# One exponential over two score banks, and one PSUM tile for seven banks, in the last attention of a four-layer kernel

## The chip, the core and the metric

The kernel runs on one core of a Trainium2 chip. Five engines matter: TensorE (products and transpositions, "PE" in the profile; its weight loads are "PEld"), VectorE ("DVE"), ScalarE ("ACT"), GpSimd ("POOL") and SyncE ("SP", which issues the transfers). TensorE writes into PSUM, which has eight banks of 512 fp32 columns on each of 128 partitions; VectorE and ScalarE read from it. The engines run side by side and wait for each other through semaphores. The metric is the device time of one execution in microseconds (us).

## What is computed

The reference takes x (16 sequences of 128 tokens, 256 features) through four layers, each an attention and a feed-forward part, both added to x. The change lies in the last layer, whose attention looks from every one of the 2048 tokens to all 2048 tokens of a context, with 16 heads of width 16 and integer-rounded q, k, v and weights:

```
attn = jnp.einsum('bhqd,bhkd->bhqk', q, k)
attn = jax.nn.softmax(attn.astype(jnp.float32), axis=-1)
attn = _fq_unsigned(attn, axis=-1)          # max/255 is the step; round to 0..255
out = jnp.einsum('bhqk,bhkd->bhqd', attn, v)
...
out = jnp.einsum over the experts: silu(x @ gate) * (x @ up) @ down, the best two of 8, and a shared one
```

The kernel gets the rounding to 0..255 by subtracting the row's maximum, adding log 255, and letting the exponential be written out as an integer.

## The kernel before

The first three layers and the keys and values of the fourth run up to about 1834 us. Then `l3` runs the last attention and the last mixture of experts together.

The work is cut into *units*: unit `u` is one tile of 128 queries and one head, 16 tiles of 16 heads, 256 in all. A unit has four *pieces* of scores, 128 x 512 each, one PSUM bank each. For a unit the steps are:

- `scores` (L967): a product per piece, TensorE.
- `peak` (L973): the negated maximum of each piece, VectorE, into a column of `nm`; `bias` (L978, L979) makes the unit's bias `nb` of the four.
- `exponentials` (L991): four exponentials, ScalarE, from the pieces' banks into the integer tile `p`, each with its sum into a column of `z`. In the profile an exponential is an ACTIVATE and an ACTIVATION_READ_ACCUMULATOR.
- `turn_p` (L1004): 16 transpositions of `p`, eight to a bank; the first eight are copied out by VectorE (L1006), the others by ScalarE (L1008).
- `values` (L1017): 16 products into the bank `av`, which is apart from the others.

Eight banks are used: one for `av`, and seven, `b0` to `b6`, for all else in the stage. `take` gives out the bank that was free longest by a hand-set due time, `give` returns it with such a time. Each take makes a new tile in the bank's own place.

The order on the engines is written out by hand (`tc.manual_schedule`): the loop over `u` issues the exponentials of `u`, pieces 2 and 3 of `u + 1` with their maxima, the transpositions of `u - 1`, the values of `u - 2`, and pieces 0 and 1 of `u + 2` with theirs. Between these stand the pieces of the rest. Ten units of each tile carry an `expert`: a gate-and-up product (L243, `gu`), two passes of ScalarE (L1192 and L1193), and `rest`, a pass of VectorE (L1196) and one of GpSimd (L1197). The table `steps` places the others (norm, projection of q, its rounding and transposition, output projection, gate, the experts' transpositions `turn_a` and `down` products) at the end of fixed units; what they read back from PSUM is put off to the middle of the next unit's exponentials (`mid`) or maxima (`between`).

The wait that an instruction gets comes from its tiles: the framework sees which tiles it reads and writes, and sets semaphores so that it comes after the earlier users of those tiles.

Of the kernel before, what the change touches and what calls it, by code (L numbers as in the profile page):

```python
# [18 lines left out]
F32 = mybir.dt.float32  # L19
# [5 lines left out]
AF = mybir.ActivationFunctionType  # L25
ALU = mybir.AluOpType
AX = mybir.AxisListType
PSUM = bass.MemoryType.PSUM

P = 128  # L30
NT = 16
D = 256
NH = 16
# [7 lines left out]
class Net:  # L41
# [879 lines left out]
    def l3(self, w3, moe_w):  # L921
# [7 lines left out]
        nc, tc = self.nc, self.tc  # L929
# [5 lines left out]
        with (self.pool("l3x", bufs=2) as pool, self.pool("l3p", bufs=3) as pp,  # L935
              self.pool("l3t", bufs=LAG + 1) as tp, self.pool("l3m", bufs=1) as mp,
              self.pool("l3e", bufs=3) as ep):
            st = {}

            banks = {f"b{j}": float(j - 7) for j in range(7)}  # L940

            def take(shape, name, dtype=F32):
                tag = min(banks, key=banks.get)
                del banks[tag]
                return self.bank(shape, tag, name, dtype), tag

            def give(tag, when):
                banks[tag] = when
# [10 lines left out]
            def flush(which, u):  # L959
                for f in which.pop(u, ()):  # L960
                    f()


            def scores(u, q):
                t, hd = divmod(u, NH)
                ps, tag = st["s", u, q] = take([P, 512], "piece")
                nc.tensor.matmul(ps, qTs[t % 2][:, hd, :],  # L967
                                 kst[q // 2][:, hd // 2, 512 * (q % 2):512 * (q % 2) + 512], start=True, stop=True)

            def peak(u, q):  # L970
                if q == 0:
                    st["nm", u] = self.s(4, "nm")
                nc.vector.tensor_reduce(st["nm", u][:, q:q + 1], st["s", u, q][0], AX.X, ALU.max, negate=True)  # L973

            def bias(u):
                t, hd = divmod(u, NH)
                nb = st["nb", u] = self.s(1, "nb")
                nc.vector.tensor_reduce(nb, st.pop(("nm", u)), AX.X, ALU.min)  # L978
                nc.vector.tensor_scalar(nb, nb, st["sq", t][:, hd:hd + 1], LN255, ALU.mult, ALU.add)  # L979

            def exponentials(u):
                t, hd = divmod(u, NH)
                if hd == 0:
                    st["z", t] = pool.tile([P, NH, 4], F32, name="z", tag="z")

                p, nb = pp.tile([P, T], I16, name="p", tag="p"), st.pop(("nb", u))
                for q in range(4):
                    if q == 2:
                        flush(mids, u)
                    ps, tag = st.pop(("s", u, q))  # L990
                    nc.scalar.activation(p[:, 512 * q:512 * q + 512], ps, AF.Exp, bias=nb,  # L991
                                         scale=st["sq", t][:, hd:hd + 1], accum_out=st["z", t][:, hd, q:q + 1])
                    give(tag, u + (0.2, 0.4, 0.6, 0.8)[q])
                st["p", u] = p

            def turn_p(u, half, now):

                if half == 0:
                    st["pT", u] = tp.tile([P, NT, P], I16, name="pT", tag="pT")
                p, out = st["p", u].bitcast(BF16), st["pT", u][:, 8 * half:8 * half + 8, :]  # L1000
                ps, tag = take([P, 8, P], "pTp", BF16)
                for j in range(8):
                    n = (8 * half + j) * P
                    nc.tensor.transpose(ps[:, j, :], p[:, n:n + P], self.identb)  # L1004
                if half == 0:
                    nc.vector.tensor_copy(out, ps.bitcast(I16))  # L1006
                else:
                    nc.scalar.copy(out.rearrange("p j q -> p (j q)").bitcast(F32), ps.rearrange("p j q -> p (j q)").bitcast(F32))  # L1008
                give(tag, now + (0.9 if half == 0 else 1.0))

            def values(u):
                t, hd = divmod(u, NH)
                if hd == 0:
                    st["av", t] = self.bank([P, NH, 16], "av", "av")
                pb = st.pop(("pT", u)).bitcast(F16)
                for c in range(NT):
                    nc.tensor.matmul(st["av", t][:, hd, :], pb[:, c, :], v[:, c, hd * 16:(hd + 1) * 16],  # L1017
                                     start=(c == 0), stop=(c == NT - 1))
# [168 lines left out]
            def expert(e):  # L1187
                def step(t, u):
                    ps, tag = take([P, 2 * IN], "gu")
                    self.matmul_acc(ps, [(st["mhT"][:, c, :], wgu[:, c, e, :]) for c in range(2)])  # L1190
                    a, b = (ep.tile([P, IN], F32, name=n, tag=n) for n in ("ma", "mb"))
                    nc.scalar.activation(a, ps[:, :IN], AF.Tanh, scale=0.5)  # L1192
                    nc.scalar.activation(b, ps[:, IN:], AF.Identity, scale=st["comb"][:, e:e + 1])  # L1193

                    def rest():
                        nc.vector.scalar_tensor_tensor(a, a, 1.0, ps[:, :IN], ALU.add, ALU.mult)  # L1196
                        nc.gpsimd.tensor_tensor(act[:, e * IN:(e + 1) * IN], a, b, ALU.mult)  # L1197
                        give(tag, u + 0.95)
                    return rest
                return step  # L1200
# [30 lines left out]
            N = NT * NH  # L1231
# [4 lines left out]
            with tc.manual_schedule(engines={E.PE, E.DVE, E.Activation, E.Pool, E.SP}):  # L1236
                nc.gpsimd.memset(act[:, NE * IN:], 0.0)
                nc.vector.tensor_scalar(sv, sv, 2.0 ** 24, None, ALU.mult)
                for qT in qTs:
                    nc.gpsimd.memset(qT, 0.0)  # L1240
                for n in sorted(n for n in steps if n < 0):
                    for f in steps[n]:
                        f(0, -2)
                        flush(mids, -1)
                        flush(betweens, -1)
                for q in range(4):
                    scores(0, q)
                    peak(0, q)
                bias(0)
                for q in range(2):  # L1250
                    scores(1, q)
                    peak(1, q)
                for u in range(N + 33):
                    if u < N:
                        exponentials(u)
                    else:
                        flush(mids, u)

                    rest = None
                    for q in (2, 3):  # L1260
                        if u + 1 < N:
                            scores(u + 1, q)
                            peak(u + 1, q)
                        if q == 2:
                            flush(betweens, u)
                            for t in range(NT):
                                if FIRST <= u - NH * t < FIRST + NE:
                                    rest = expert(u - NH * t - FIRST)(t, u)
                    if u + 1 < N:
                        bias(u + 1)  # L1270

                    if 0 <= u - 1 < N:
                        for half in range(2):
                            turn_p(u - 1, half, u)
                    if 0 <= u - LAG < N:
                        values(u - LAG)
                        if (u - LAG) % NH == NH - 1:
                            divide((u - LAG) // NH, u)
                    for q in range(2):
                        if u + 2 < N:  # L1280
                            scores(u + 2, q)
                    if rest:
                        rest()
                    for q in range(2):
                        if u + 2 < N:
                            peak(u + 2, q)

                    for t in reversed(range(NT)):
                        for f in steps.get(u - NH * t, ()) if u - NH * t >= 0 or t > 0 else ():
                            f(t, u)  # L1290


    def run(self):
        self.load_x()
        late = ExitStack()
        self.l0(late)
        with self.pool("w3", 1) as self.w:
            w3 = self.l3_weights()
            self.middle(w3)
            late.close()  # L1300
            with self.pool("w4", 1, "right") as self.w:
                moe_w = self.moe_weights("L3_ffn", 10)
                with self.psum(av=1, **{f"b{j}": 1 for j in range(7)}):
                    self.l3(w3, moe_w)


# [67 lines left out]
```

## Time and profile before

| | |
|---|---|
| three runs | 3094.66, 3092.42, 3086.54 us; median 3092.42 |
| profiled execution | 3084.17 us, span 3082.5 us, mean granted TensorE clock 0.958 |
| TensorE products, weight loads | busy 2613.2 us (85%), 1772.8 us (58%) |
| VectorE | busy 2116.1 us (69%) |
| ScalarE | busy 1893.2 us (61%) |
| GpSimd | busy 1060.0 us (34%) |
| DMA | 12 GB/s on average |

The busy shares are means over the whole span, with stages of different limits in it. The last stage, from 1834 us, has its own balance, and is to be read by a window. Rows of the profile give line, engine, operation, output<-input, shapes and count; then busy us and mean ns of one, then the idle time before it and whose end ended it. PEclk is the clock that TensorE was granted, 1.00 at full speed.

### The profile page before, as it was taken

What the parts mean: (1) busy time and instruction counts of PE and PEld (TensorE: products, weight loads), DVE (VectorE), ACT (ScalarE), POOL (GpSimd) and SP (SyncE); (2) the same over time, 40 slices, a digit from 0 to 9 for tenths busy, and PEclk for the clock granted to TensorE, in tenths of its full rate; (3) what the DMA queues carried; (4) which work ended last, traced back from release to release, by engine and by line L of the source; (5) the groups of instructions that cost most, each with busy time, mean ns of one, the idle gap of its engine ahead of it and who ended that gap; (6) DMA issues with size and microseconds to landing.
All of it is one profiled execution on the core that took longest, in us unless ns stands there. A gap on an engine that the chain in (4) does not pass through costs nothing.

```text
span 3082.5 us, 50232 instructions
## 1 busy us (share of the span) xinstructions
PE 2613.2 (85%) x18166; PEld 1772.8 (58%) x18166; DVE 2116.1 (69%) x5254; ACT 1893.2 (61%) x4908; POOL 1060.0 (34%) x1683
## 2 busy tenths in 40 slices
PE   5889999999998877888888857788888888888888
PEld 3556666666665544555555534555555555555556
DVE  5655565656657435667666539888888888888884
ACT  1344444444444325555555429988888888888895
POOL 4544443444443315555555420222222222222212
PEclk9899999999998988999999979999999999999999
DMA  5000000000001010000000010000000000000000
GB/s 200 1 1 1 1 1 1 1 1 1 1 1 53 21 54 5 5 4 5 5 4 3 1 71 1 2 3 3 3 3 3 3 3 3 3 3 3 3 3 6
DMA packets 27385, 37.68 MB, mean 12 GB/s; under 512 B 6432, under 2 KB 23424, under 8 KB 26368
## 3 DMA queue, kind: packets, MB, share of 16 engines
q1 hardware_dynamic: 27136, 34.47, 3.4%
q8 instruction: 143, 2.34, 0.3%
q14 instruction: 106, 0.87, 0.1%
HBM read 32.37 MB, written 2.10 MB: 11 GB/s over the span
## 4 chain that ended last, share of the span: by engine, by line
PE 53%; DVE 19%; ACT 17%; POOL 6%; issue 5%; DMA 1%; ACTq 0%; SPq 0%; DVEq 0%; POOLq 0%
ACT p L991 10%; PE gu L243 9%; PE tp L219 6%; DVE nm L973 5%; PE pTp L1004 4%; PE oproj L549 4%; PE q L243 4%; PE scores L273 4%; PE moe L1214 3%; PE av L289 3%; PE piece L967 3%; PE moe L243 2%; PE oT L541 2%; DVE pT L1006 2%; PE out L243 2%
## 5 line engine op out<-in xcount | busy, mean ns | idle before, releaser
L991 ACT ACTIVATE p<-piece,nb,hs 128x512 int16<-128x512 f32 x1024 | 789.4, 785 | 8.1 <-DVE nb L979 8.1
L973 DVE TENSOR_REDUCE nm<-piece 128x1 f32<-128x512 f32 x1024 | 661.6, 683 | 141.5 <-PE piece L967 138.8
L967 PE MATMUL piece<-kst,qT 128*128 128x512 bf16 x1024 | 351.5, 383 | 127.2 <-DVE pT L1006 96.7
L1004 PEld LDWEIGHTS <-p 128*128 128x128 bf16 x4096 | 257.8, 98 | 193.2 <-issue 160.6
L1004 PE MATMUL pTp<-identb,p 128*128 128x128 bf16 x4096 | 294.5, 220 | 51.6 <-ACT p L991 28.5
L243 PE MATMUL gu<-w_L_ffn_wgu,mhT 128*128 128x352 f32 x640 | 223.2, 474 | 21.4 <-ACT p L991 19.1
L1197 POOL TENSOR_TENSOR act<-ma,mb 128x176 f32<-128x176 f32 x160 | 89.5, 559 | 421.3 <-DVE ma L1196 390.7
L235 ACT COPY pT<-tp 128x512 f32<-128x512 f32 (+1 forms) x208 | 116.0, 563 | 181.0 <-PE tp L219 180.0
L1008 ACT COPY pT<-pTp 128x512 f32<-128x512 f32 x256 | 150.0, 586 | 107.7 <-PE pTp L1004 107.7
L991 ACT ACTIVATION_READ_ACCUMULATOR p<-piece,nb,hs 128x1 f32 x1024 | 214.1, 209 | 0.0
L270 POOL TENSOR_TENSOR kx<-kT,hmask 128x512 f32<-128x512 f32 x128 | 132.9, 1047 | 146.0 <-PE scores L273 94.4
L534 ACT ACTIVATE s<-s,nb,qs 128x128 f32<-128x128 f32 x256 | 123.2, 482 | 97.4 <-DVE nb L532 95.9
L289 PEld LDWEIGHTS av<-v,pT 128*128 128x128 f32 x1024 | 132.4, 197 | 87.1 <-ACT pT L235 73.6
L1006 DVE COPY pT<-pTp 128x1024 int16<-128x1024 int16 x256 | 174.3, 681 | 1.4 <-PE pTp L1004 1.4
L243 PE MATMUL gu<-w_L_ffn_wgu,hT 128*128 128x352 f32 x512 | 174.5, 463 | 0.9 <-ACT actT L235 0.6
L289 PE MATMUL av<-v,pT 128*128 128x17 f32 x1024 | 133.7, 262 | 47.8 <-ACT pT L235 47.7
L243 PEld LDWEIGHTS gu<-w_L_ffn_wgu,mhT 128*128 128x128 f32 x640 | 111.9, 189 | 101.7 <-ACT p L991 63.5
L280 ACT ACTIVATE p<-scores,mx,qs 128x128 f32<-128x128 f32 x256 | 96.9, 459 | 118.7 <-DVE mx L278 111.1
L967 PEld LDWEIGHTS <-qT 128*128 128x128 bf16 x1024 | 91.8, 98 | 130.8 <-issue 104.6
L275 DVE TENSOR_REDUCE mx<-scores 128x4 f32<-128x512 f32 x128 | 88.2, 689 | 114.0 <-PE scores L273 113.5
L273 PE MATMUL scores<-kx,qT 128*128 128x512 f32 x256 | 152.2, 679 | 3.1 <-ACT qT L235 2.7
L1179 POOL TENSOR_SCALAR gw<-gtop,gden 128x2 f32<-128x2 f32 x16 | 4.2, 263 | 417.3 <-DVE gden L1178 417.3
(367 smaller groups left out, 5973.3 us busy)
## 6 DMA issues: line engine op xcount, KB each, us to landing
w_L_ffn_wgu<-in_L_ffn_wgu SPq DMA_DIRECT2D x1, 3520.0 KB, 11.7
w_L_ffn_wgu<-in_L_ffn_wgu SPq DMA_DIRECT2D x1, 2816.0 KB, 11.3
x<-in_x SPq DMA_DIRECT2D x16, 128.0 KB, 4.2
ctxT<-in_ctxT SPq DMA_DIRECT2D x4, 512.0 KB, 5.1
w_L_ffn_qT<-in_L_ffn_qT SPq DMA_DIRECT2D x1, 2048.0 KB, 12.2
w_L_ffn_oT<-in_L_ffn_oT SPq DMA_DIRECT2D x1, 2048.0 KB, 17.5
ctx<-in_ctx SPq DMA_DIRECT2D x16, 128.0 KB, 2.0
out<-x SPq DMA_DIRECT2D x16, 128.0 KB, 1.7
```

The lines of the kernel that those rows point to most:

```text
L219: nc.tensor.transpose(ps[:, j, :], src[:, (j0 + j) * P:(j0 + j + 1) * P], self.ident)
L243: self.nc.tensor.matmul(ps, a, b, start=(j == 0), stop=(j == n - 1))
L270: nc.gpsimd.tensor_tensor(kx, kT[oc].unsqueeze(1).to_broadcast([P, 4, P]), self.hmask[:, hs].unsqueeze(2).to_broadcast([P, 4, P]), ALU.mult)
L273: nc.tensor.matmul(ps, qT[:, oc, :], kx, start=True, stop=True)
L289: nc.tensor.matmul(av[:, 4 * g + h, :], pT[:, h, :], v[:, 4 * g + h, :], start=True, stop=True)
L549: nc.tensor.matmul(proj, oT[:, j, :], w["o"][:, c, :], start=(c == 0), stop=(c == 15))
L967: nc.tensor.matmul(ps, qTs[t % 2][:, hd, :], kst[q // 2][:, hd // 2, 512 * (q % 2):512 * (q % 2) + 512], start=True, stop=True)
L973: nc.vector.tensor_reduce(st["nm", u][:, q:q + 1], st["s", u, q][0], AX.X, ALU.max, negate=True)
L991: nc.scalar.activation(p[:, 512 * q:512 * q + 512], ps, AF.Exp, bias=nb, scale=st["sq", t][:, hd:hd + 1], accum_out=st["z", t][:, hd, q:q ...
L1004: nc.tensor.transpose(ps[:, j, :], p[:, n:n + P], self.identb)
L1006: nc.vector.tensor_copy(out, ps.bitcast(I16))
L1008: nc.scalar.copy(out.rearrange("p j q -> p (j q)").bitcast(F32), ps.rearrange("p j q -> p (j q)").bitcast(F32))
```

## The change

The seven banks become one tile, `seven`, of 7 x 512 columns; `take` gives out slices of it, numbered 0 to 6. With that, a pair of pieces can be one operand even where its two banks do not touch: `pair` makes an access pattern over banks `a` and `b` with step `abs(a - b)`. A unit's exponentials become two, of 1024 columns each, over pieces 0 and 1 and over pieces 2 and 3; the maxima of pieces 0 and 1 become one; pieces 2 and 3 keep one each. Where the first piece of a pair lies in the higher bank, the pair is read in the other order, and `turn_p` turns the two halves in the other order to make up for it.

```diff
-            banks = {f"b{j}": float(j - 7) for j in range(7)}
+            seven = self.bank([P, 7, 512], "seven", "piece")
+            banks = {j: float(j - 7) for j in range(7)}
 
             def take(shape, name, dtype=F32):
                 tag = min(banks, key=banks.get)
                 del banks[tag]
-                return self.bank(shape, tag, name, dtype), tag
+                ps = seven[:, tag, :]
+                if dtype != F32:
+                    ps = ps.bitcast(dtype)
+                n = shape[1] * (shape[2] if len(shape) == 3 else 1)
+                ps = ps[:, :n]
+                return ps.rearrange("p (j q) -> p j q", q=shape[2]) if len(shape) == 3 else ps, tag
+
+            def pair(u, q):
+
+                a, b = st["s", u, q][1], st["s", u, q + 1][1]
+                return seven[:, min(a, b):max(a, b) + 1:abs(a - b), :], a < b
...
             def peak(u, q):
                 if q == 0:
-                    st["nm", u] = self.s(4, "nm")
-                nc.vector.tensor_reduce(st["nm", u][:, q:q + 1], st["s", u, q][0], AX.X, ALU.max, negate=True)
+
+                    st["nm", u] = self.s(3, "nm")
+                    nc.vector.tensor_reduce(st["nm", u][:, :1], pair(u, 0)[0], AX.XY, ALU.max, negate=True)
+                else:
+                    nc.vector.tensor_reduce(st["nm", u][:, q - 1:q], st["s", u, q][0], AX.X, ALU.max, negate=True)
...
-                    st["z", t] = pool.tile([P, NH, 4], F32, name="z", tag="z")
+                    st["z", t] = pool.tile([P, NH, 2], F32, name="z", tag="z")
 
                 p, nb = pp.tile([P, T], I16, name="p", tag="p"), st.pop(("nb", u))
-                for q in range(4):
+                for q in (0, 2):
                     if q == 2:
                         flush(mids, u)
-                    ps, tag = st.pop(("s", u, q))
-                    nc.scalar.activation(p[:, 512 * q:512 * q + 512], ps, AF.Exp, bias=nb,
-                                         scale=st["sq", t][:, hd:hd + 1], accum_out=st["z", t][:, hd, q:q + 1])
-                    give(tag, u + (0.2, 0.4, 0.6, 0.8)[q])
+                    ps, st["first", u, q // 2] = pair(u, q)
+                    nc.scalar.activation(p[:, 512 * q:512 * q + 1024].rearrange("p (a n) -> p a n", a=2), ps, AF.Exp,
+                                         bias=nb, scale=st["sq", t][:, hd:hd + 1],
+                                         accum_out=st["z", t][:, hd, q // 2:q // 2 + 1])
+                    for k in (0, 1):
+                        give(st.pop(("s", u, q + k))[1], u + (0.3, 0.31, 0.7, 0.71)[q + k])
...
                 ps, tag = take([P, 8, P], "pTp", BF16)
+                first = st.pop(("first", u, half))
                 for j in range(8):
-                    n = (8 * half + j) * P
+                    n = (8 * half + (j if first else (j + 4) % 8)) * P
                     nc.tensor.transpose(ps[:, j, :], p[:, n:n + P], self.identb)
...
                 for q in range(4):
                     scores(0, q)
+                for q in (0, 2, 3):
                     peak(0, q)
                 bias(0)
                 for q in range(2):
                     scores(1, q)
-                    peak(1, q)
+                peak(1, 0)
...
-                    for q in range(2):
-                        if u + 2 < N:
-                            peak(u + 2, q)
+                    if u + 2 < N:
+                        peak(u + 2, 0)
...
-                with self.psum(av=1, **{f"b{j}": 1 for j in range(7)}):
+                with self.psum(av=1, seven=1):
                     self.l3(w3, moe_w)
```

In the changed kernel the lines are: pieces L978, maxima L985 (pair) and L987, bias L992 and L993, exponentials L1005, transpositions L1021 with their copies L1023 and L1025, values L1034, the expert's passes L1209, L1210 and L1213.

## The prediction

> **What bounds the kernel now.** The page's first two parts give the whole. Then the windows view cuts out the stage that the change touches, from 1834 us (the first score product starts at 1835.8) to the end, 1248.5 us.
>
> ```profile
> span 3082.5 us, 50232 instructions
> PE 2613.2 (85%) x18166; PEld 1772.8 (58%) x18166; DVE 2116.1 (69%) x5254; ACT 1893.2 (61%) x4908; POOL 1060.0 (34%) x1683
> 1834.00:3035.00 1201.00, 1000.42 (x10718) 690.16 (x10719) 1023.13 (x2335) 1066.93 (x2761) 234.66 (x426) 0.99 0.01 3
> L991 ACT ACTIVATE p<-piece,nb,hs 128x512 int16<-128x512 f32 x1024 | 789.4, 785 | 8.1 <-DVE nb L979 8.1
> L973 DVE TENSOR_REDUCE nm<-piece 128x1 f32<-128x512 f32 x1024 | 661.6, 683 | 141.5 <-PE piece L967 138.8
> L1008 ACT COPY pT<-pTp 128x512 f32<-128x512 f32 x256 | 150.0, 586 | 107.7 <-PE pTp L1004 107.7
> ```
>
> In 1201 us there are 256 units (a tile of 128 queries by a head), so one takes 4.69 us. ScalarE is busy 89% of it, VectorE 85%, TensorE 83%. That three engines are this full together is the point: they work on different banks at once. ScalarE waits little (8.1 us before its exponentials, 107.7 us before its copies), so ScalarE is the first bound, VectorE just behind it. A stretch of the timeline shows it:
>
> ```profile
> 2402.70 0.38 PE L967 MATMUL piece<-kst,qT 128*128 128x512 bf16 x1 [0.25 <-ACT p L991]
> 2403.00 0.80 ACT L991 ACTIVATE p<-piece,nb,hs 128x512 int16<-128x512 f32 x1
> 2403.17 0.61 PE L1004 MATMUL pTp<-identb,p 128*128 128x128 bf16 x8
> 2403.67 0.22 ACT L991 ACTIVATION_READ_ACCUMULATOR p<-piece,nb,hs 128x1 f32 x1
> 2403.76 0.80 ACT L991 ACTIVATE p<-piece,nb,hs 128x512 int16<-128x512 f32 x1
> ...
> 2404.16 0.68 DVE L1006 COPY pT<-pTp 128x1024 int16<-128x1024 int16 x1
> ```
>
> TensorE transposes into one bank while ScalarE reads another. Exponentials follow each other in 0.76 us (2403.00 to 2403.76); a wait of TensorE on ScalarE is over when the accumulator has been read, 0.05 us before.
>
> **The change, part by part.**
>
> *Fewer, larger instructions.* Per unit four exponentials become two of 1024 columns. L991 has 785 ns at 512 columns, L280 459 ns at 128, so a column costs 0.85 ns: 785+435 = 1220 ns. Start to start that is 1.19 us, so ScalarE is spared 4x0.755-2x1.19 = 0.64 us. Two maxima (1.29 us together in the timeline) become one: 683 ns at 512 columns and 155 ns at 8 (the gate's maximum) give 1.06 ns a column, 1224 ns; VectorE is spared 0.07 us. The minimum over 3 values instead of 4 is nothing. No row has a 1024-column read out of two separate banks. Below, nothing suggests that it is cheaper than contiguous; above, 2x785 would bring ScalarE's gain to zero. I take the slope.
>
> *Seven tiles become one.* This decides. Before, each bank was a tile of its own, and a writer waited only for that tile's readers. Now every product, transposition, maximum, copy and exponential of the stage has the one tile `seven` as operand. The instruction list that the changed kernel builds to, with each instruction's waits, reads on TensorE, for one unit with an expert, shortened:
>
> ```
> L978  piece (pieces 0, 1 of u+2)    [waits Activation]   x2, the second without a wait
> L978  piece (piece 2 of u+1)        [waits Activation]
> L243  piece (expert's gate and up)  [waits DVE]
> L978  piece (piece 3 of u+1)        [waits Activation]
> L1021 piece (8 transpositions)      [waits DVE]
> L1021 piece (8 transpositions)      [waits DVE]
> ```
>
> Followed to the semaphores' counts, each is a wait for the last access to `seven` that stands before it in the program, whatever its bank: piece 2 waits for the second exponential, though its bank went free with the first; the expert's product waits for the maximum of piece 2, in another bank; the second eight transpositions wait for VectorE's copy of the first eight. The first exponential of u+1 waits for the pair's maximum of u+2, a read against a read. All 8784 accesses, in 3416 runs of one engine after another, stand in one order, and never do two of the three engines work on `seven` at the same time. The change of the transposition order (`first`) and the times in `give` only pick banks, and cost nothing here.
>
> The chain of a unit with an expert is then: two exponentials; piece 2; its maximum; gate and up; tanh and scaling; piece 3; its maximum; 8 transpositions; VectorE's copy; 8 transpositions; ScalarE's copy; two pieces; `rest` and the pair's maximum; next unit. I sum it over the stage.
>
> - ScalarE: 256 x (1.19+1.22+0.085, to the end of the accumulator's read) = 639; 256 copies x 0.586 = 150; 160 x 0.67 for L1192 and L1193 = 107; the copies between the exponentials (48 of 0.59, 48 of 0.37, 32 of 0.57, 32 of 0.38) about 70. Together 966 us.
> - VectorE: 510 maxima x 0.681 = 347; 256 x 1.224 = 313; 256 copies x 0.681 = 174; 160 x 0.327 = 52; the additions and copies of the steps (48+16+16+16 near 0.41, 32 of 0.43) about 52. Together 939 us.
> - TensorE at full clock: 512 x 0.61 for eight transpositions = 312; 510 single pieces x 0.377 = 192; 255 pairs x 0.60 = 153; 160 gate-and-up of 1.36 = 218; down products 32 x 2.4 and 16 x 1.9 = 107; projections, gate and other transpositions 106. Together 1088 us.
> - 3416 handovers. In the timeline a waiting engine starts 0.03 to 0.09 us after the releaser's end; at 0.06, 205 us.
>
> Sum 3198 us instead of 1248.5. The values' products (L1017, 0.55 us per unit) read no bank of `seven` and stay beside ScalarE's copy; the two small bias operations of VectorE (0.44 us) stay beside the transpositions (0.61 us); POOL's and SP's work has no such operand, and their lists are not rearranged.
>
> *TensorE's clock.* In this chain TensorE works 1088+140 of 3198 us, 38%, and between a unit's last piece and the next piece 2 it idles through 1.2 to 1.5 us of VectorE and 2.5 us of ScalarE. What that does to the clock is in the trace, in windows of 3.41 us (columns: us, PE busy, PEclk, DMA share, GB/s):
>
> ```profile
> 1783.04:1786.45 3.41, 1.13 (x4) 1.00 0.00 0
> 1786.45:1789.87 3.42, 0.00 (x0) 0.50 0.00 0
> ...
> 1806.93:1810.35 3.42, 0.94 (x3) 1.00 0.00 0
> 1810.35:1813.76 3.41, 0.00 (x0) 0.50 0.00 0
> ...
> 1841.07:1844.48 3.41, 2.62 (x8) 0.50 0.00 0
> 1844.48:1847.89 3.41, 3.25 (x22) 0.50 0.00 0
> 1847.89:1851.31 3.42, 2.36 (x36) 1.00 0.02 5
> ```
>
> A window with about a third of TensorE busy is followed by one at half clock, and at half clock even 2.62 of 3.41 us busy was not enough to rise, 3.25 us was. Over the whole span, all 18 full-clock windows under 40% busy were followed by half clock, and no half-clock window under 80% busy (22) by full clock. The Trainium skill, "TensorE: Matmul & The Clock Gate", section on the HAM clock gate, puts it otherwise: half clock after at least one idle window of about 3.4 us. By that rule a gap of 3.9 to 4.1 us holds a whole window in roughly one unit of six, and the stage would run mostly at full clock: 3198 us or a little more. By the trace's rows it drops at once and seldom returns. I go by the rows.
>
> At half clock the trace has 0.58 for a piece, 1.06 for two, 1.86 for 16 transpositions (so 1.01 for 8), 2.07 for four 128x256 fp32 products (1.03 before). TensorE's sum becomes 517+296+268+400 (gate and up at 2.5)+221 (down)+194 = 1896 us, and the values' products then outlast ScalarE's copy by some 0.15 us, 40 us. Sum at half clock 4046 us. Long runs on TensorE (down products, transpositions-values-pieces) will lift some windows; at 13% full clock the stage takes 3936 us.
>
> The profiled execution was 3084.2 us (span 3082.5); 3084.2-1248.5+3936 = 5772. The median of the runs lies 8 us above it: 5780.
>
> **The rivals.**
>
> *Serial, clock held.* As the page's rule has it: 3084+8-1248+3198 = 5042 us, in mixtures up to 5300. For it: long gaps here are rarely wholly empty windows. Against: the 18 of 18.
>
> *Only part is serial.* If the waits bound only neighbouring or enclosed banks, half of the added 1950 us would stay, about 4070. Against: the counts, which spare no bank.
>
> *Faster.* The Trainium skill, "PSUM — Partial Sum Buffer", on bank collisions, asks for order between engines by bank and quadrant, not by more. If the program that runs were ordered so, the tile's merging would cost nothing, and ScalarE's 0.64 us a unit would be gained until VectorE (4.00-0.07 us busy of 4.69) stops it: between 0 and 164 us, with half of it 3010. It decides from the point where a write to one bank need not await a reader of another. The trace shows that banks do work side by side (the second fence), but the changed kernel's waits do not allow it. By the page's rule 3010, by the built waits 5780; I go by the waits.
>
> *The change not doing what it says:* the two exponentials are there in the list, 512 of 1024 columns, and 256 maxima over two banks.
>
> **How the numbers follow.** Serial at mostly half clock 0.68 (5450 to 6150: handovers at 0.1 us add 137, and as much may be missed in the half-clock sums); serial with the clock mostly held 0.26 (5000 to 5450); part serial 0.03; faster 0.03. Predicted 5780. The range 5100 to 6150 leaves out the last two, the bottom of the second and a little above: under 0.2. Changes under 0.3% (9 us) could not be told from none here. Faster by more 0.03, within 0.01 (the low end of the faster case), slower 0.96.
>
> **What would show it.** Right: the stage lasts over 3 ms; each of PE, DVE and ACT is busy under 50% of it, and their sums near the span; PEclk near 5 in the last two thirds of the page's slices; the exponentials near 1220 ns; large idle entries piece<-exponential, maximum<-piece, transpositions<-DVE copy. The clock row alone separates 5780 from 5042. Wrong: busy shares that still sum to well over the span in this stage, or exponentials far from 1220 ns.

## The result, and the profile after

The changed kernel takes 5818.98 us (median of four runs, 5813.3 to 5827.55) against 3093.54 us before (four runs, 3086.54 to 3095.84): 1.882 times as long, 95% interval 1.8781 to 1.8858. The forecast was 5780. First the page of the changed kernel: span, busy times, and the granted clock in 40 slices of the span.

```profile
span 5811.6 us, 48916 instructions
PE 3509.7 (60%) x18023; PEld 2171.0 (37%) x18166; DVE 2163.4 (37%) x4998; ACT 1757.8 (30%) x3884; POOL 1057.5 (18%) x1683
PEclk9999999899996555555555555555555555555556
```

VectorE is busy a little longer than before (2116.1 us then), ScalarE a little shorter (1893.2), and the span has nearly doubled: most of the added time is waiting. TensorE's busy time grew by 900 us with the same products, and the last row says why: from slice 13 on it ran at about half clock. The window over the last stage (columns: length; busy time and count of PE, PEld, DVE, ACT, POOL; clock, DMA share, GB/s):

```profile
1834.00:5811.60 3977.60, 1943.93 (x10807) 1123.66 (x10934) 1082.07 (x2122) 949.85 (x1791) 248.40 (x454) 0.51 0.00 1
```

The stage went from 1248.5 to 3977.6 us; the first 1834 us did not change. PE, DVE and ACT together are busy 3976 us, where before three such numbers added up to 2.5 times the stage. That this sum is the stage itself is partly chance: it holds work that lies beside the line of turns (the values' products and the bias), and lacks the handovers. The same window for the instructions that touch `seven` alone (columns as above, without POOL) is the stricter view:

```profile
1834.00:5811.60 3977.60, 1838.36 (x6711) 427.55 (x1594) 929.41 (x1327) 946.67 (x1759) 0.51 0.00 1
```

PE, DVE and ACT have 3714.4 us together here, and laid over each other by their starts and ends in the trace they overlap for 0.0 us: no two engines ever work on `seven` at the same time. The costliest groups (count | busy, mean ns | idle time before them, and whose end ended most of it):

```profile
L978 PE MATMUL piece<-kst,qT 128*128 128x512 bf16 x897 | 500.8, 588 | 1079.0 <-ACT p L1005 788.0
L987 DVE TENSOR_REDUCE nm<-piece 128x1 f32<-128x512 f32 x512 | 354.2, 692 | 1850.9 <-PE piece L978 1850.9
L1005 ACT ACTIVATE p<-piece,nb,hs 128x1024 int16<-128x1024 f32 x512 | 615.5, 1204 | 1042.6 <-PE piece L1055 311.4
L1021 PE MATMUL piece<-identb,p 128*128 128x128 bf16 x4096 | 517.3, 306 | 402.7 <-DVE pT L1023 200.2
L1025 ACT COPY pT<-piece 128x512 f32<-128x512 f32 x256 | 150.0, 586 | 1269.0 <-PE piece L1021 1269.0
L985 DVE TENSOR_REDUCE nm<-piece 128x1 f32<-128x1024 f32 x256 | 312.6, 1221 | 328.9 <-PE piece L978 166.3
```

Before, the exponentials had 8.1 us of idle time ahead of them, the maxima 141.5, the copies 107.7. Now it is 1042.6, 1850.9 + 328.9 and 1269.0. The wide instructions themselves cost what was expected: 1204 and 1221 ns. A unit with an expert in the timeline (start, duration, in brackets the idle time and the releaser), without the rows of weight loads:

```profile
3611.02 0.20 ACT L1005 ACTIVATION_READ_ACCUMULATOR p<-piece,nb,hs 128x1 f32 x1
3611.26 0.58 PE L978 MATMUL piece<-kst,qT 128*128 128x512 bf16 x1 [3.10 <-ACT p L1005]
3611.89 0.69 DVE L987 TENSOR_REDUCE nm<-piece 128x1 f32<-128x512 f32 x1 [4.36 <-PE piece L978]
...
3613.07 2.71 PE L243 MATMUL piece<-w_L_ffn_wgu,mhT 128*128 128x352 f32 x4 [1.23 <-DVE qT L1103]
...
3618.96 0.69 DVE L1023 COPY pT<-piece 128x1024 int16<-128x1024 int16 x1 [0.66 <-PE piece L1021]
3619.70 1.01 PE L1021 MATMUL piece<-identb,p 128*128 128x128 bf16 x8 [0.78 <-DVE pT L1023]
...
3620.80 0.59 ACT L1025 COPY pT<-piece 128x512 f32<-128x512 f32 x1 [4.30 <-PE piece L1021]
...
3621.43 1.01 PE L978 MATMUL piece<-kst,qT 128*128 128x512 bf16 x2 [0.31 <-ACT pT L1025]
```

Each row that waited for another engine starts 0.04 to 0.09 us after the end of its releaser, whether the two share a bank or not. The second eight transpositions (3619.70) write a bank that VectorE's copy (3618.96 to 3619.65) does not touch, and wait for it all the same.

### The profile page after: what moved, and what is told of

It reads as the page before. It is cut to its first block, busy times and chain, and to the rows that moved or that the text cites. A ratio compares the mean times of both kernels' runs of the same rounds, so it can differ in the third digit from the quotient of the medians.

```text
span 5811.6 us, 48916 instructions
## 1 busy us (share of the span) xinstructions
PE 3509.7 (60%) x18023; PEld 2171.0 (37%) x18166; DVE 2163.4 (37%) x4998; ACT 1757.8 (30%) x3884; POOL 1057.5 (18%) x1683
## 4 chain that ended last, share of the span: by engine, by line
PE 28%; DVE 16%; ACT 15%; another core or an unknown queue 6%; issue 2%; ACTq 0%; DVEq 0%
ACT p L1005 11%; PE piece L243 9%; PE piece L978 7%; PE piece L1021 7%; DVE nm L987 6%; DVE nm L985 5%; PE piece L1231 3%; DVE pT L1023 3%; PE piece L1055 1%; ACT pT L1025 1%; DVE ma L1213 1%; ACT ma L1209 1%; ACT mb L1210 1%; ACT aT L1059 0%
## 5 line engine op out<-in xcount | busy, mean ns | idle before, releaser
L978 PE MATMUL piece<-kst,qT 128*128 128x512 bf16 x897 | 500.8, 588 | 1079.0 <-ACT p L1005 788.0
L987 DVE TENSOR_REDUCE nm<-piece 128x1 f32<-128x512 f32 x512 | 354.2, 692 | 1850.9 <-PE piece L978 1850.9
L1005 ACT ACTIVATE p<-piece,nb,hs 128x1024 int16<-128x1024 f32 x512 | 615.5, 1204 | 1042.6 <-PE piece L1055 311.4
L1021 PEld LDWEIGHTS <-p 128*128 128x128 bf16 x4096 | 433.1, 140 | 919.2 <-issue 919.0
L1021 PE MATMUL piece<-identb,p 128*128 128x128 bf16 x4096 | 517.3, 306 | 402.7 <-DVE pT L1023 200.2
L1025 ACT COPY pT<-piece 128x512 f32<-128x512 f32 x256 | 150.0, 586 | 1269.0 <-PE piece L1021 1269.0
L243 PE MATMUL piece<-w_L_ffn_wgu,mhT 128*128 128x352 f32 x640 | 429.1, 825 | 153.0 <-DVE nm L987 57.2
L243 PEld LDWEIGHTS piece<-w_L_ffn_wgu,mhT 128*128 128x128 f32 x640 | 185.7, 320 | 760.5 <-DVE nm L987 327.9
L985 DVE TENSOR_REDUCE nm<-piece 128x1 f32<-128x1024 f32 x256 | 312.6, 1221 | 328.9 <-PE piece L978 166.3
L978 PEld LDWEIGHTS <-qT 128*128 128x128 bf16 x1024 | 125.2, 122 | 579.5 <-issue 481.7
L1209 ACT ACTIVATE ma<-piece 128x176 f32<-128x176 f32 x160 | 50.8, 318 | 683.3 <-PE piece L243 683.3
L1023 DVE COPY pT<-piece 128x1024 int16<-128x1024 int16 x256 | 177.1, 692 | 172.1 <-PE piece L1021 172.1
L1231 PE MATMUL piece<-w_L_ffn_wd,aT 128*128 128x256 f32 x448 | 197.6, 622 | 65.0 <-DVE nm L985 61.0
L1213 DVE SCALAR_TENSOR_TENSOR ma<-ma,piece 128x176 f32<-128x176 f32 x160 | 54.1, 338 | 448.8 <-remote 203.3
L1034 PEld LDWEIGHTS <-pT 128*128 128x128 f16 x4096 | 160.5, 109 | 0.7 <-issue 0.7
```

What stands on the lines that cost most here:

```text
L243: self.nc.tensor.matmul(ps, a, b, start=(j == 0), stop=(j == n - 1))
L978: nc.tensor.matmul(ps, qTs[t % 2][:, hd, :], kst[q // 2][:, hd // 2, 512 * (q % 2):512 * (q % 2) + 512], start=True, stop=True)
L985: nc.vector.tensor_reduce(st["nm", u][:, :1], pair(u, 0)[0], AX.XY, ALU.max, negate=True)
L987: nc.vector.tensor_reduce(st["nm", u][:, q - 1:q], st["s", u, q][0], AX.X, ALU.max, negate=True)
L1005: nc.scalar.activation(p[:, 512 * q:512 * q + 1024].rearrange("p (a n) -> p a n", a=2), ps, AF.Exp, bias=nb, scale=st["sq", t][:, hd:hd + ...
L1231: nc.tensor.matmul(ps, st["aT", c // 4][:r, c % 4, :], wd[:r, c, :], start=(c == c0), stop=(c == c1 - 1))
```

## The experiments

The theory has two parts: one tile for seven banks makes the engines take turns whatever the bank, and the turns leave TensorE so idle that its clock falls to half. Rivals: the wide instructions, or the banks picked for them, are to blame; and the clock follows something else. Where only one run was made (`e1_merge`, `e3_fill`, `e4_fixed`, `e6_fill2`), no ratio is given.

**Merging alone (`e1_merge`).** The instructions of before; only the tile is changed.

```diff
-            banks = {f"b{j}": float(j - 7) for j in range(7)}
+            seven = self.bank([P, 7, 512], "seven", "piece")
+            banks = {j: float(j - 7) for j in range(7)}
...
-                return self.bank(shape, tag, name, dtype), tag
+                ps = seven[:, tag, :]
...
```

> The kernel before with one edit: its seven one-bank tiles b0 to b6 become the seven banks of one tile, as in the change; its instructions stay as they are, four exponentials of 512 columns and four maxima a unit. Theory (one tile makes the engines take turns, whatever the bank): slower than the changed kernel, because four short exponentials (4 x 0.755 = 3.02 us) stand for two wide ones (2.41 us) and two short maxima for the pair's, all on the one line of turns: about 5819 + 256 x 0.7 = 5990 us. Rival (the wide instructions or their two-bank operands cost it, the merged tile does not): about 3093 us.

Measured: 6008.91 us, clock 0.51 in the stage. The wide instructions did not cause the loss. On the line of turns they even save 190 us, near the 179 us (256 x 0.7) of the expectation.

**The choice of banks (`e4_fixed`).** The changed kernel, with pieces always in one of three fixed pairs.

```diff
-                tag = min(banks, key=banks.get)
-                del banks[tag]
+                if name != "piece":
+                    tag = min(banks, key=banks.get)
+                    del banks[tag]
+                elif "second" in st:
+                    tag = st.pop("second")
+                else:
+                    tag = min((j for j in (0, 2, 4) if j in banks and j + 1 in banks),
+                              key=lambda j: max(banks[j], banks[j + 1]))
+                    st["second"] = tag + 1
+                    del banks[tag], banks[tag + 1]
```

> The changed kernel with only the other edit of the kernel with waits by bank: pieces are always given one of the bank pairs 0-1, 2-3, 4-5; waits stay by tile. Theory (only the waits matter): 5819 us within 0.5%. Rival (the choice of banks is what frees the other kernel): far below 5000 us.

Measured: 5812.21 us, no difference. With one order for all banks, it does not matter which is picked.

**Waits by bank (`e2_bank`, `e5_bank2`).** The same instructions, fixed pairs and tile; every instruction on `seven` now waits for the last users of its own banks (`users`) on the other engines, and otherwise only for instructions with which it shares another tile (`kin`, by the tiles' names).

```diff
+            def on(ins, *tags):
...
+                    before = list({j.name: j for b in tags for j in users.get(b, {}).values()}.values())
+                    names = {x.bass_ap.tensor.name for x in [*i.ins, *i.outs] if getattr(x, "bass_ap", None) is not None}
+                    names = {n for n in names if not n.startswith("piece")}
+                    keep = {j.name: j for j in before}
...
+                            keep.update({j.name: j for j in kin.get(m, ())})
...
+                            tc.declare_no_dep(i, group=other, reason="by bank",
+                                              keep=[j for j in keep.values() if other in str(j.engine)])
+                    for j in before:
+                        if j.engine != i.engine:
+                            tc.add_manual_dep(i, j.name, mybir.DependencyInfo(mybir.DependencyClass.Sync,
+                                              mybir.DependencyReason.DATA), reason="by bank")
...
-                    nc.vector.tensor_reduce(st["nm", u][:, :1], pair(u, 0)[0], AX.XY, ALU.max, negate=True)
+                    on(nc.vector.tensor_reduce(st["nm", u][:, :1], pair(u, 0)[0], AX.XY, ALU.max, negate=True),
+                       st["s", u, 0][1], st["s", u, 1][1])
```

> The changed kernel's instructions on the same seven-bank tile, with the waits on that tile set by the bank that an instruction touches instead of by the tile. So that a wide instruction touches only its own two banks, pieces 0 and 1, and 2 and 3, are always given one of the bank pairs 0-1, 2-3, 4-5. Theory (order by tile is the whole loss): back to the level of the kernel before, 2950 to 3100 us. Rival (wide exponentials and maxima lengthen the chain in themselves, or two-bank reads collide with products): well above 3300 us.

Measured: 3501.68 us, ratio to before 1.1334 (1.1309 to 1.1358). Most of the loss is gone, but the theory's range is missed, and the time lies where the rival had it. The view of waits of this kernel (total us, times, longest) shows one that no bank explains:

```profile
ACT pT L1069 <- DVE pT L1067: 377.4, 216, 5.2
```

VectorE's and ScalarE's copies write separate halves of one SBUF tile `pT`, and the `keep` list of this edit, which goes by tile names, had put them in order. So this wait is the edit's own: the kernel before does not have it. There VectorE's copy runs from 2404.16 to 2404.84, and ScalarE's into the other half starts under it:

```profile
2404.64 0.59 ACT L1008 COPY pT<-pTp 128x512 f32<-128x512 f32 x1
```

`e5_bank2` takes this pair off the list:

```diff
-                            keep.update({j.name: j for j in kin.get(m, ())})
+                            keep.update({j.name: j for j in kin.get(m, ()) if n[:3] != "pT_" or "PE" in str(i.engine) + str(j.engine)})
```

> The kernel with waits by bank, less one wait: there ScalarE's copy of the second transposed half still waited for VectorE's copy of the first (429.3 us of idle time before it in all), because both write one tile pT, in separate halves, and an order kept for a shared tile was kept whole. Here that wait is gone. Theory (only waits across engines that the data do not need cost time): 3502 - 256 x 1.4 = about 3140 us, and 3000 to 3150 us. Rival (the wide instructions cost the remaining 410 us): about 3450 to 3500 us.

Measured: 3316.84 us, ratio 1.0752 (1.0721 to 1.0782). The wait is gone (the copies now wait for their transpositions, 230.4 us), but only 185 of the expected 360 us came back, which is between the two expectations: with it gone, other waits end last. Reading two banks beside busy neighbours does not lengthen the wide instructions: their means are 1209 and 1224 ns here, 1204 and 1221 in turns. Its stage:

```profile
1834.00:3315.00 1481.00, 1081.50 (x10776) 755.03 (x10938) 1024.52 (x2122) 933.13 (x1791) 250.84 (x456) 0.93 0.01 3
```

1481 us instead of 3978, with the same instructions: the engines' sum is 2.05 times the stage, and the clock is at 0.93. On `seven`, TensorE and ScalarE now work at the same time for 573 us, where the changed kernel has 0.0. Waits by tile, and the clock that they bring down, are at least 5819 - 3317 = 2500 us of the 2725 (the fixed pairs, as shown below, cost something themselves).

**The clock (`e3_fill`, `e6_fill2`).** The changed kernel with all its turns, and products that nothing reads in TensorE's idle stretches.

```diff
+            def fill(n):
+                for _ in range(n if "avb" in st else 0):
+                    nc.tensor.matmul(st["avb"][:, 256:], self.identb, kst[0][:, 0, :256], start=True, stop=True)
...
                             scores(u + 1, q)
+                            fill(4)
                             peak(u + 1, q)
...
+                    fill(20)
                     if rest:
```

> The changed kernel with all its turns kept, and idle stretches of TensorE filled with products that nothing reads (20 of 256 columns after pieces 0 and 1 of a unit, 4 after each other step), written to the unused half of the values' bank. Theory (half of the lengthening beyond the turns is TensorE at half clock, because it is busy too little): the clock of the last stage stays near full and the time falls to about 5000 to 5100 us (the forecast's case with the clock held was 5042). Rival (the clock follows something else, or does not matter): half clock or an unchanged time of 5800 us or more.

Measured: 5406.0 us, 413 less, and between the two expectations. Its windows of 3.41 us show why (columns as above):

```profile
3593.17:3596.59 3.42, 2.06 (x15) 1.60 (x14) 1.34 (x4) 1.27 (x3) 2.26 (x6) 1.00 0.00 0
3596.59:3600.00 3.41, 1.47 (x7) 0.87 (x7) 1.02 (x2) 1.21 (x3) 2.35 (x3) 1.00 0.02 5
3600.00:3603.41 3.41, 3.41 (x12) 1.81 (x11) 0.60 (x1) 0.62 (x2) 0.00 (x0) 0.50 0.00 0
3603.41:3606.82 3.41, 3.01 (x45) 2.42 (x44) 1.15 (x4) 0.59 (x1) 0.00 (x0) 1.00 0.00 0
```

In these rows a window with TensorE busy 60% keeps the clock; the next, 43%, loses it; a full one (3.41 of 3.41) gets it back. Gaps of up to 3.17 us during the exponentials kept costing such windows, and 20 products in a row held the unit's last step back. `e6_fill2` puts 8 of them ahead of that step and 20 behind it.

> The changed kernel with filling products again, spread otherwise: in the first filled kernel 20 of them in a row (2.2 us) stood ahead of the step that ends a unit and held it back by about 1.4 us, while TensorE still idled 3.1 us during the exponentials. Now 8 stand ahead of that step and 20 behind it. Theory (the clock's share of the loss is 700 to 800 us): clock of the last stage above 0.9 and 5000 to 5100 us. Rival (its share is what the first filled kernel showed, about 400 us): about 5400 us with the same clock.

Measured: 5116.65 us, just above the theory's range. Its stage:

```profile
1834.00:5114.90 3280.90, 2565.32 (x23409) 1938.74 (x23662) 1081.90 (x2122) 948.88 (x1791) 250.62 (x457) 0.99 0.01 2
```

At a clock of 0.99, with the turns kept and 12600 products more, the stage takes 3281 us. So the clock's share of the loss is at least 702 us: TensorE's work on `seven` alone shrank from 1838 to 1063 us in the traces, and the filling took some of that back. The forecast's sum for turns at full clock (3198) is 83 us short of a stage that also carries the filling.

**What the last 230 us are (`e8_before_fixed`, `e9_early`).** The kernel before, seven tiles and single exponentials, with the fixed pairs of `e4_fixed` alone (its due times for exponentials become 0.3, 0.31, 0.7, 0.71):

> The kernel before, seven tiles and one-bank instructions, with the choice of banks alone changed to the fixed pairs 0-1, 2-3, 4-5 for pieces. It asks what the last 230 us of the kernel with waits by bank are (3317 against 3087). Theory A (the fixed pairs: every other step's bank is number 6, so a gate-and-up product waits for VectorE's addition of the step before): 3200 to 3300 us. Theory B (a wide exponential frees its first bank only with its second, so pieces 2 and 3 start 0.7 us later and everything behind them): 3080 to 3130 us here.

Measured: 3265.03 us, ratio 1.0565 (1.0547 to 1.0582). That is 175 us, as much as three quarters of the 230. Its timeline shows a place:

```profile
2608.74 0.41 DVE L1225 TENSOR_TENSOR x<-moe,x 128x256 f32<-128x256 f32 x1
...
2609.21 1.45 PE L243 MATMUL gu<-w_L_ffn_wgu,mhT 128*128 128x352 f32 x4 [1.11 <-DVE x L1225]
```

Bank 6 is the only one outside the pairs; the gate-and-up product got the bank of the last step's result, and waits until VectorE has read it. `e9_early` has waits by bank and fixed pairs, gives bank 6 to the steps alone, and empties it sooner:

```diff
+                    tag = 6 if name != "pTp" else min((j for j in range(6) if j in banks), key=banks.get)
...
                     rest = None
+                    flush(betweens, u)
                     for q in (2, 3):
...
                         if q == 2:
-                            flush(betweens, u)
```

> The changed kernel with waits by bank and fixed pairs (3317 us), and bank 6 kept for the steps outside attention and freed earlier: VectorE's work on a step's result (the addition after a projection, the lower copy of q) comes ahead of the maximum of piece 2 instead of behind it, and transpositions take banks of pairs only. Theory A: the waits of gate-and-up products and transpositions on those VectorE results (42 + 28 + 17 + 16 + 26 + 13 us in the trace) go, about 3317 - 140 = 3180 us. Theory B: at most 30 us gained, 3290 us or more.

Measured: 3325.89 us, 9 above `e5_bank2`: theory B. The waits that theory A named fell from 143 to 53 us, and others took their place: the transpositions wait 52.2 us for exponentials instead of 22.0, the pieces 105.9 instead of 51.2 for VectorE's copy. A sum of waits in a trace is not what their removal gives.

**Without fixed pairs (`e12_narrow`, `e13_plain`, `e10_near`, `e11_near2`).** `e12_narrow` has the merged tile and waits by bank, with the bank choice and single instructions of before.

> The instructions of the kernel before, its choice of banks and its order, on the seven-bank tile, with waits by bank (and one memset of the sums per tile on GpSimd, 16 in all). It differs from the first experiment (seven banks merged, 6009 us) in the waits alone. Theory (order by tile is the whole loss): 3080 to 3110 us, that is the kernel before. Rival (an operand inside a seven-bank tile costs something besides the order): above 3150 us.

Measured: 3172.36 us, ratio 1.0261 (1.0236 to 1.0286), above the theory's range and inside the rival's. The view of waits has one that this kernel brought along, GpSimd's memset of the sums:

```profile
ACT p L1061 <- POOL z L1040: 45.8, 13, 3.5
```

`e13_plain` leaves the memset out:

```diff
-                    nc.gpsimd.memset(st["z", t], 0.0)
```

> The narrow kernel with waits by bank (3172 us) without the 16 memsets of the exponentials' sums, which all its exponentials write anyway. In its trace ScalarE's exponentials waited 45.8 us for those memsets (13 of 16 tiles in view), because GpSimd had them in its queue behind a normalization. Theory (the 84 us above the kernel before are those memsets and some leftover waits): 3172 - 16 x 3.5 = 3116 us, and 3090 to 3125 us. Rival (an operand in the merged tile costs something besides the order): 3150 us or more.

Measured: 3119.1 us, ratio 1.0109 (1.0082 to 1.0135), as the theory had it. This kernel and `e1_merge` have the same instructions on the same tile with the same choice of banks; only the waits differ, and it is 3119 against 6009 us. Its stage:

```profile
1834.00:3116.60 1282.60, 1061.16 (x10938) 720.30 (x10938) 1039.72 (x2379) 1086.82 (x2815) 252.99 (x461) 0.97 0.01 4
```

What is left above before, 28 us, was not traced further; other orders that the `keep` list adds may be the rest, which is not shown.

`e10_near` and `e11_near2` ask whether wide instructions pay once the waits go by bank and the banks are not tied. The second piece takes a neighbouring bank if one is free soon enough, and only such pairs get wide instructions (here `e10_near`; `e11_near2` has `(2,)` for `(0, 2)` and no wide maxima):

```diff
+                if name == "piece" and "first" in st:
+                    a = st.pop("first")
+                    near = [j for j in (a - 1, a + 1) if j in banks and banks[j] <= banks[tag] + 0.4]
+                    tag = min(near, key=banks.get) if near else tag
...
+            def near(u, q):
+                return abs(st["s", u, q][1] - st["s", u, q + 1][1]) == 1
...
+                    if h in (0, 2) and near(u, h) if q % 2 == 0 else st.get("wide"):
```

> Waits by bank, and the wide instructions only where they cost no bank: the second piece of a pair takes a neighbouring bank if one is free and at most 0.4 of a unit later than the earliest; 370 of 512 pairs get one wide exponential and 196 of 256 one wide maximum, the others two of 512 columns. Theory (fixed pairs cost 175 us, and wide exponentials about 50 more by freeing banks late): 3090 to 3160 us. Rival (with the banks free to choose, ScalarE's 0.3 us less a pair pay): below 3075 us.

> As the kernel before it in this call, with wide exponentials for pieces 2 and 3 only (177 of 256 units) and maxima of 512 columns. The banks of pieces 0 and 1, which the next unit's pieces 2 and 3 wait for, come free as early as before. Theory: ScalarE spares 177 x 0.3 = 53 us that are partly on the path, 3050 to 3090 us. Rival (a wide exponential holds back the first half's bank for the transpositions as much as it saves): 3090 us or more.

Measured: 3240.49 us (ratio 1.0477, 1.0454 to 1.05) and 3229.13 us (1.0443, 1.0424 to 1.0462). The first missed both of its ranges, the second lies where the rival had it. Both carry the memset, which cost 53 us between `e12_narrow` and `e13_plain`; with as much taken off, an estimate, they would stand near 3187 and 3176, still 68 and 57 us above `e13_plain`. What ScalarE saved, it waited for: it is busy 975 and 1030 us in the stage against 1087 in `e13_plain`, and from 2000 us to near the end its copies wait 236 and 208 us for transpositions against 102. Wider instructions did not pay here either, though part of that may be the preference for neighbouring banks. No version beat the kernel before.

## Why the prediction was right, point by point

- *Durations of the wide instructions.* 1220 and 1224 ns were taken from slopes; measured 1204 and 1221.
- *One order for all accesses.* Right: on `seven` the three engines overlap for 0.0 us, in `e1_merge`, `e4_fixed`, `e3_fill` and `e6_fill2` too, and `e13_plain` against `e1_merge` shows the waits by tile as the cause. To the 3714 us of the trace come 75 us for 127 of 1024 pieces that it lacks. That makes 3789 us on the line and leaves 188 us for 3416 handovers, 0.055 us each; the forecast took 0.06.
- *TensorE's clock.* The reading of the trace's rows held: 0.51 was granted, where the forecast allowed a mean of 0.565 (13% at full clock). Of the long runs that were to lift it, the ones of transpositions, values and pieces never did. The down products did: after 18 windows filled with them, at 84 to 100% busy, the clock was full, and mostly for a single window (columns: length, PE busy, clock, DMA share, GB/s):

```profile
2709.46:2712.88 3.42, 3.04 (x7) 0.50 0.00 0
2712.88:2716.29 3.41, 0.81 (x3) 1.00 0.00 0
2716.29:2719.70 3.41, 2.33 (x4) 0.50 0.11 38
```

  The working of the case with the clock held (5042) took one row of the Trainium skill's table ("TensorE: Matmul & The Clock Gate", section on the HAM clock gate), half clock after an idle window, and left out the next: full clock comes back only after a busy window of about 3.4 us. Outside the down products no window at half clock was more than 85% busy, so by both rows together this kernel too stays mostly at half clock. Where the page and the runs part is how the clock is lost: none of the 206 windows that lost it in `e3_fill` was idle throughout (last section).
- *Terms of the sum.* At half clock throughout the forecast had 4046, 68 too many. TensorE on the line came to 1838 + 75 = 1913 (1896 forecast; gate and up took 429 instead of 400), VectorE to 929 (939), ScalarE to 947 (966), the handovers to 188 (205). The 40 us for values outlasting ScalarE's copy were not there: in the timeline the copy ends at 3621.39 and the piece starts at 3621.43. The share at full clock took 110 us off the forecast, and hardly any of it was granted. These misses offset each other: that 3936 is so close to 3978 is partly luck.
- *Clock held (5042).* As an experiment this case exists, at 5117 with filling. As a forecast for this kernel it was wrong.
- *Part serial.* Fell: no two engines overlap on any banks of `seven`, and the choice of banks changed nothing (`e4_fixed`).
- *Faster, by order per bank (3010).* The order by bank, which the Trainium skill's "PSUM — Partial Sum Buffer" asks for (section on bank collisions), does bring the stage back, but not below before: 3317 with fixed pairs. The step that fails in this rival is the gain. ScalarE has 152 us less to do in `e5_bank2` than before (933 against 1085), and none of it shows: with the same fixed pairs and single exponentials, `e8_before_fixed` is 52 us faster. ScalarE waits instead: for transpositions ahead of its copies 230.4 us (143.8 in `e8_before_fixed`, 100.8 before), for gate-and-up products 224.4 (123.9 and 20.6). That a wide exponential frees its first bank only with its second may be the reason; no run separates that. ScalarE is the busiest engine before, and still not a bound that alone sets the time.

## What to carry to other kernels

A tile can be the unit of waiting as well as of memory: merging the PSUM buffers so that an instruction can span two of them tied the order of everything that uses any of them, and this showed in the waits of the built program before anything ran. It does not hold of every tile, and the account of the waits ahead of the prediction is too wide there: the two copies into the SBUF tile `pT` overlap in the kernel before. Read a stage by the instructions that touch the shared tile: where those of different engines never overlap in time, the engines take turns. And price the clock with the waits: here at least 702 of 2725 us came only from TensorE being busy too little.

## What the hardware showed that was not expected

The clock was lost without an idle window. In `e3_fill`, cut into windows of 3.41 us in the clock's own phase from 1900 us on: 206 windows at full clock with TensorE busy 8 to 47% were followed by half clock, and 557 with 42 to 100% by full clock. At half clock, 206 windows with 85 to 100% were followed by full clock, and 54 with 59 to 84% by half clock. Not one of the windows that lost the clock was wholly idle, and no gap of TensorE in that stretch is longer than 3.17 us, so none would be with another start either. In this run, then, TensorE held its clock from some 45% busy on and regained it only from about 85%: it sat at half clock with loads at which it had held full clock.

These two limits are of this run, and not a rule. In the last stage of the kernel before, four windows of 66 to 69%, with no gap over 0.49 us, were followed by half clock, one of them here (columns as in the last fence):

```profile
2178.99:2182.40 3.41, 2.33 (x32) 1.00 0.00 0
2182.40:2185.81 3.41, 3.41 (x36) 0.50 0.03 10
```

In `e6_fill2` the five that lost it were 50% busy, and in `e5_bank2` one of 79% regained it. So the busy share that the profile shows is not all that the clock follows; what else it is stays open. What the runs do show is the price: 12600 products that nothing reads (TensorE busy 78% of the stage) held the clock at 0.99 and brought 702 us.
